# A convolution and attention hybrid: weighted sums two tiles behind, a norm in steps, leftovers at later pieces, a bias row on two row groups

## The chip, the core and the metric

The kernel runs on one core of a Trainium2 chip. A core has five engines with a queue each, which work at the same time and meet at semaphores: TensorE (PE in the profile, with its weight loads as PEld) multiplies matrices into PSUM, ScalarE (ACT) evaluates functions, VectorE (DVE) does elementwise work, reductions and 32x32 block transposes, GpSimd (POOL) does elementwise work and copies between partitions, SyncE (SP) issues most of the loads and stores. Each engine takes its instructions in order. SBUF has 128 partitions.

The metric is the device time of one execution in microseconds (us). A profile is one execution of its own; its times are read from the first instruction on.

## The reference

Input x is (4, 128, 64, 64): four images (N) of 128 channels and 4096 pixels, which later are tokens. Cut to what matters:

```python
# layer 0
g  = group_norm(x)                                   # 32 groups of 4 channels
e1 = prelu(w1 @ g + b1); e2 = prelu(w2 @ g + b2)     # 64 channels each
a  = prelu(wa @ g + ba)                              # 128 channels
x  = x + einsum('nij,ncj->nci', softmax(einsum('nci,ncj->nij', e1, e2), axis=2), a)
# layer 1, on tokens t: (4, 4096, 128)
u  = ln(t)
z  = cos(heads(u) + rx) and its running products     # 16 heads of 8
q  = ring(z)
ctx = softmax(q @ q.T / sqrt(8)) @ q                 # keys, queries and values are the same q
x1 = ln(u + ctx @ w_comb.T + b_comb)
f  = relu((cos(x1[..., :8]) * cos(ry)) @ f1.T + fb1) @ f2.T + fb2
t  = t + ln(x1 + f)
# layer 2: Wx = batch_norm(ln(t) @ W.T); y_k = sigmoid(Wx_k + y_(k-1) @ V.T); t = t + y
```

## The kernel before

**Stages.** The loop at the end of the kernel takes the images one after the other. For each, `first_stage` does layer 0 (`layer0`) and between its pieces the feed-forward of the image before; `second_stage` does the attention (`attention`). After the fourth image `third_stage` does the last feed-forward, and the recurrence over tokens follows. Inside the stages the order of the instructions on TensorE, ScalarE and VectorE is the order in which the code is written; in the attention that holds for GpSimd too. Where one stage follows another, a planner may mix the instructions of both ends.

**The convolutions.** `layer0` first normalises x (L327, eight parts), then makes e1 and e2 in eight pieces: two matmuls (L339) into a pair of PSUM banks, two activations on ScalarE (L291, L292), one operation on VectorE (L293). Then come four pieces of `asmT`: for each of two banks a bias matmul of one row (L347), then sixteen instructions of `wa` (L356) on top of it, then two operations on VectorE (L297, L298). After each of these twelve pieces, and after each score piece later, it calls `meanwhile`, which takes one leftover of the attention before, if there is any, a step of the image's own tokens, and a step of the feed-forward of the image before (`step_late`). A feed-forward is started on the first call and another every fifteen calls, at most two at a time. Its third step computes the statistics of `v`, with a power on GpSimd (r_v, in `rsqrt`, L225), and its fifth uses them on VectorE (L252).

**The attention.** Keys, queries and values are the same matrix, so the scores are symmetric, and the kernel computes each tile of 128 keys by 1024 queries only once where it can. For each of eight pairs of heads there are four blocks of 1024 queries. A block works through its own eight key tiles and through the tiles of the next one or two blocks: blocks 0 and 1 have 24 tiles (two foreign, one own, and so on), blocks 2 and 3 have 16 (one foreign, one own). Each tile is one turn of the loop (L823):

- scores: four matmuls on four row groups (L833) into two buffers of `ps_pair` (three in all);
- two exponentials on ScalarE (L842); for a foreign tile with a sum over the row (an accumulator read follows). The result goes into `exps` (six buffers) or into unused parts of `xs`, five turns deep;
- `run_pending`: mirror steps (L693), which use transposed foreign tiles as weights for the other block. Four foreign tiles make a group of sixteen steps; `credit` says how many are taken in a turn;
- `weigh` (L711): the weighted sum of the tile before, into the one accumulator of the block (`ps_acc`). After a block's last tile `finish` (L735) transposes the accumulator into `o` (L739), copies it on GpSimd into `own` (L747, sixteen copies) and puts two functions into `ends`: `mirrored` (`by_token` L732, `turned` L759 on VectorE, `other` L766 on GpSimd, sums into `own`) and `result` (reciprocal L773 and product L774 on VectorE);
- `run_flips`: transposes of foreign tiles on VectorE (L680), not on the last tile of a block.

At the end of an image the last two `result` functions are handed on as `left`. In the last block of an image three functions prepare the next one (`upcoming`): at the third tile the loads of x (`load_x`), at the fifteenth the eight `bn_stats` of `norm_stats` (L304) and their aggregate, and behind the last tile the two matmuls over groups (L309, L317) and the power r_g. `turned` has one buffer, `other` one of its own.

**Memory.** The stages' pools stand one behind another in SBUF from the left or the right. What a stage writes waits for the readers of what stood at the same place. In the attention, `queries`, `fixed` (q_aug and mirror), `keys` stand in this order; in an even image `flipped` stands at the right end.

Of the kernel before, what the change touches and what calls it, by code (L numbers as in the profile page):

```python
# [10 lines left out]
F32 = mybir.dt.float32  # L11
# [15 lines left out]
def kernel(  # L27
# [45 lines left out]
    TG = 4  # L73
# [84 lines left out]
    ba_row = load(ba, "ba_row")  # L158
# [141 lines left out]
    def norm_stats(n, xs):  # L300

        st = once.tile([P, NIC, 6], F32, tag="gst", name=f"gst{n}")
        for i in range(NIC):
            nc.vector.bn_stats(st[:, i, :], xs[:, ts(i, IC)])  # L304
        mv = once.tile([P, 2], F32, tag="gmv", name=f"gmv{n}")
        nc.vector.bn_aggr(mv, st)
        yield
# [7 lines left out]
        nc.vector.scalar_tensor_tensor(tv, dm, dm, mv[:, 1:2], ALU.mult, ALU.add)  # L315
        pv = get("ps_tok", f"pv{n}")
# [3 lines left out]
    def layer0(n, xs, xh, norm, shifted, begin, meanwhile):  # L320
# [23 lines left out]
        for i in range(NIC // 2):  # L344
            pc = pair_psum(f"pa{n}_{i}")
            for j in range(2):
                nc.tensor.matmul(  # L347
                    pc[:, j, :],
                    ones[0:1, :],
                    ba_row.unsqueeze(1).broadcast_to([1, TG, P]),  # L350
                    start=True,
                    stop=False,
                    skip_group_check=True,
                )
# [106 lines left out]
    def tokens(im, i, sums):  # L461
# [26 lines left out]
        by_token = small.tile([P, P], F32, tag="sums", name=f"sums{n}_{i}")  # L488
# [66 lines left out]
    def attention(n, q, xs, tail, upcoming):  # L555
# [152 lines left out]
        def weigh(it):  # L708
            for h in range(2):
                for x in range(2):  # L710
                    nc.tensor.matmul(  # L711
                        it["acc"][ts(2 * h + x, 32), :],
# [22 lines left out]
        def finish(pair, b, acc, later, denom):  # L735
# [3 lines left out]
            nc.vector.transpose(o, acc)  # L739
# [11 lines left out]
            def mirrored():  # L751
# [9 lines left out]
                other = once.tile([P, QT * 2 * D], F32, tag="other", name=f"other{n}_{pair}_{b}")  # L761
# [42 lines left out]
        before = None  # L804
# [8 lines left out]
        for pair in range(NPAIR):  # L813
            keys, queries, qa, later, denom = ready
            for b in range(NQB):
                acc = get("ps_acc", f"acc{n}_{pair}_{b}")
# [6 lines left out]
                for at, jt in enumerate(tiles):  # L823
# [30 lines left out]
                    if at == 1:  # L854
                        credit = max(credit, 3.0)
                    credit -= run_pending(turn, int(credit))
# [3 lines left out]
                    if before is not None:  # L860
                        weigh(before)
                        if before["last"]:
                            finish(*before["block"])
# [29 lines left out]
                    if jt != tiles[-1]:  # L893
                        run_flips(2)
# [3 lines left out]
                    if end_of_all and at in (2, QT + 6) and upcoming:  # L898
                        upcoming.pop(0)()
                    before = {  # L900
                        "acc": acc,
# [5 lines left out]
                        "block": (pair, b, acc, later, denom),  # L907
                    }
                assert not coming
# [3 lines left out]
        weigh(before)  # L913
        finish(*before["block"])
        while flips or pending:
            run_flips(TG)
            run_pending(turn + 2, 16)
        for f in upcoming:
            f()
# [217 lines left out]
    def first_stage(im, before):  # L1137
# [11 lines left out]
        with stage(f"conv{n}", **pools, **psum), tc.manual_schedule(engines=engines):  # L1149
            nc.vector.memset(get("gap", f"gap{n}")[:, 0:1], 0.0)  # L1150
            own = []
            step_late = in_steps(feed_forwards(before) if before else [], 15, 2)

            def meanwhile(steps=1):
                if before and before["left"]:
                    before["left"].pop(0)()
# [24 lines left out]
    def second_stage(im, tail, upcoming):  # L1181
# [3 lines left out]
            queries=((P, IC), 6),  # L1185
            fixed=((P,), 1),
            keys=((P, QB), 6),
# [4 lines left out]
            turned=((P, 2 * P), 1),  # L1192
# [6 lines left out]
        sides = {"flipped": "right"}  # L1199
        if im["side"] == "right":  # L1200
            sides = {}
# [48 lines left out]
    x_next = {"xs": load_x(0, ts(0, P))}  # L1250
    for n in range(N):
# [4 lines left out]
        upcoming = []  # L1256
        if n + 1 < N:
            upcoming = [
                lambda: x_next.update(xs=load_x(n + 1, ts(n + 1, P))),
                lambda: x_next.update(norm=norm_stats(n + 1, x_next["xs"])) or next(x_next["norm"]),  # L1260
                lambda: x_next.update(norm=next(x_next["norm"])),
            ]
# [112 lines left out]
    with tc.If(any_bad > 0):  # L1375
        with tc.For_i(0, N * P, P) as r0:
            image = open_image("r", ds(r0, P), "left", load_x("r", ds(r0, P)))
            second_stage(image, first_stage(image, None), [])
# [101 lines left out]
```

## Time and profile before

| | us |
|---|---|
| median of 3 runs (lowest, highest) | 7468.12 (7465.14, 7470.33) |
| the profiled execution's own time | 7473.21 |
| its span, first to last instruction | 7471.5 |
| mean granted clock of TensorE | 0.976 of full |

Among the costliest groups of instructions are:

| line, engine, what | count | busy us | mean ns |
|---|---|---|---|
| L842 ACT, exponentials into `exps` | 3144 | 3096.7 | 1036 |
| L842 ACT, exponentials into `xs` | 1976 | 1958.5 | 1036 |
| L680 DVE, transposes of foreign tiles | 3072 | 2221.8 + 1375.4 | 1216, 1214 |
| L693 PE, mirror steps | 49152 | 1867.8 | 279 |
| L711 PE, weighted sums | 20480 | 1683.9 + 1055.7 | 595, 594 |
| L833 PE, attention scores | 10240 | 1309.8 | 495 |
| L347 PE, bias of the value convolution | 64 | 42.9 | 802 |
| L304 DVE, statistics of x | 32 | 19.7 | 677 |

A line of a timeline gives the start and the length in us, the engine, the source line, the operation, the tile written and the tiles read, the shape, and how many instructions are merged; in brackets stands how long the engine was idle before and what ended that. Matmuls overlap, so for TensorE the distance from start to start says more than a length. A fp32 matmul counts as two instructions. A line of the waits gives the engine, what it was about to write, what it waited for, and the sum, the number and the longest of such waits. A window line gives the stretch, its length, the busy time of each engine with the instructions in it, the granted clock of TensorE (1.00 is full), the share of the DMA engines and GB/s.

### The profile page before, as it was taken

What the parts mean: (1) busy time and instruction counts of PE and PEld (TensorE: products, weight loads), DVE (VectorE), ACT (ScalarE), POOL (GpSimd) and SP (SyncE); (2) the same over time, 40 slices, a digit from 0 to 9 for tenths busy, and PEclk for the clock granted to TensorE, in tenths of its full rate; (3) what the DMA queues carried; (4) which work ended last, traced back from release to release, by engine and by line L of the source; (5) the groups of instructions that cost most, each with busy time, mean ns of one, the idle gap of its engine ahead of it and who ended that gap; (6) DMA issues with size and microseconds to landing.
All of it is one profiled execution on the core that took longest, in us unless ns stands there. A gap on an engine that the chain in (4) does not pass through costs nothing. (4 is left out here: it accounts for less than half of the span.)

```text
span 7471.5 us, 212466 instructions
## 1 busy us (share of the span) xinstructions
PE 7212.8 (97%) x88078; PEld 3317.1 (44%) x88078; DVE 5435.5 (73%) x7364; ACT 6104.6 (82%) x9557; POOL 2718.0 (36%) x9768
## 2 busy tenths in 40 slices
PE   8999999999999999999899999999999999999977
PEld 3434444444444444444444444444444444444446
DVE  4677777775777777777677777777667777777764
ACT  3479999995448999999344999999844599999975
POOL 1024443342224444343323433444322343444342
PEclk9999999999999999999899999999999999999978
DMA  0010000000111000000011100000001100000012
GB/s 26 26 43 22 23 25 21 19 9 22 36 45 37 26 19 21 23 23 17 15 36 46 36 21 19 23 24 18 18 20 40 43 30 21 23 23 26 11 58 102
DMA packets 81506, 211.99 MB, mean 28 GB/s; under 512 B 8769, under 2 KB 8801, under 8 KB 79761
## 3 DMA queue, kind: packets, MB, share of 16 engines
q1 hardware_dynamic: 77312, 186.68, 7.3%
q8 instruction: 693, 11.35, 0.6%
q10 hardware_dynamic: 2016, 10.49, 0.3%
q14 instruction: 285, 2.33, 0.1%
q0 software_dynamic: 1200, 1.14, 0.1%
HBM read 141.65 MB, written 56.62 MB: 27 GB/s over the span
## 5 line engine op out<-in xcount | busy, mean ns | idle before, releaser
L842 ACT ACTIVATE e<-s 128x1024 f32<-128x1024 f32 x3144 | 3096.7, 1036 | 25.3 <-PE s L833 15.2
L680 DVE STREAM_TRANSPOSE t<-e 128x1024 f32<-128x1024 f32 x1896 | 2221.8, 1216 | 496.0 <-ACT e L842 495.4
L842 ACT ACTIVATE xs<-s 128x1024 f32<-128x1024 f32 x1976 | 1958.5, 1036 | 17.5 <-PE s L833 5.5
L693 PE MATMUL misc<-t,mirror 128*32 128x128 f32 x49152 | 1867.8, 279 | 12.5 <-DVE later L704 11.4
L711 PE MATMUL acc<-e,q_aug 128*32 128x512 f32 x12576 | 1683.9, 595 | 0.0
L680 DVE STREAM_TRANSPOSE t<-xs 128x1024 f32<-128x1024 f32 x1176 | 1375.4, 1214 | 352.1 <-ACT xs L842 351.5
L693 PEld LDWEIGHTS misc<-t,mirror 128*32 128x32 f32 x49152 | 1200.2, 110 | 623.5 <-issue 598.8
L833 PEld LDWEIGHTS s<-queries,keys 32*128 32x128 f32 x10240 | 497.2, 182 | 2165.5 <-issue 1804.3
L747 POOL COPY own<-o 32x36 f32<-32x36 f32 x2048 | 428.3, 209 | 2622.3 <-DVE o L739 2542.3
L833 PE MATMUL s<-queries,keys 32*128 32x512 f32 x10240 | 1309.8, 495 | 17.2 <-ACT e L842 11.6
L711 PE MATMUL acc<-xs,q_aug 128*32 128x512 f32 x7904 | 1055.7, 594 | 0.0
L403 PE MATMUL acc<-p,asmT 128*128 128x512 f32 x2048 | 983.0, 612 | 0.0
L388 ACT ACTIVATE p<-s 128x1024 f32<-128x1024 f32 x512 | 497.1, 1022 | 569.3 <-PE s L380 562.3
L396 DVE TENSOR_TENSOR total<-total,p 128x1024 f32<-128x1024 f32 x448 | 575.7, 1285 | 296.8 <-ACT p L388 273.0
L650 POOL COPY mirror<-q 32x128 f32<-32x128 f32 x2048 | 604.8, 295 | 112.6 <-PE misc L693 22.9
L403 PEld LDWEIGHTS acc<-p,asmT 128*128 128x128 f32 x2048 | 360.9, 192 | 516.8 <-issue 514.5
L380 PE MATMUL s<-e,e 64*128 64x512 f32 x2048 | 524.2, 630 | 3.9 <-DVE asmT L298 3.7
L766 POOL COPY other<-turned 32x64 f32<-32x64 f32 x2048 | 470.7, 230 | 87.3
L711 PEld LDWEIGHTS acc<-e,q_aug 128*32 128x32 f32 x12576 | 396.1, 110 | 33.6 <-ACT e L842 18.9
L842 ACT ACTIVATION_READ_ACCUMULATOR e<-s 128x1 f32 x1896 | 406.5, 214 | 0.0
L380 PEld LDWEIGHTS s<-e,e 64*128 64x128 f32 x2048 | 180.8, 191 | 277.1 <-issue 262.3
L711 PEld LDWEIGHTS acc<-xs,q_aug 128*32 128x32 f32 x7904 | 249.3, 110 | 18.3 <-ACT xs L842 8.7
(243 smaller groups left out, 4742.9 us busy)
## 6 DMA issues: line engine op xcount, KB each, us to landing
keys<-parts_dram SPq DMA_DIRECT2D x256, 256.0 KB
queries<-parts_dram SPq DMA_DIRECT2D x1024, 32.0 KB
fx<-x_dram SPq DMA_DIRECT2D x64, 256.0 KB
x_dram<-x SPq DMA_DIRECT2D x56, 256.0 KB
xs<-in_x_dram SPq DMA_DIRECT2D x16, 512.0 KB
t_dram<-t2T SPq DMA_DIRECT2D x32, 256.0 KB
t2s<-t_dram SPq DMA_DIRECT2D x16, 512.0 KB
parts_dram<-high SPq DMA_DIRECT2D x28, 256.0 KB
```

Source lines behind the costliest of these rows:

```text
L380: nc.tensor.matmul(s[:, j, :], e2[rows, ts(2 * jp + j, P)], e1[rows, ts(ic, IC)], start=True, stop=True,)
L388: nc.scalar.activation(p, s, AF.Exp)
L396: nc.vector.tensor_tensor(state[ic], state[ic], p, ALU.add)
L403: nc.tensor.matmul(state["acc", ic], asmT[:, ts(2 * jp + j, P)], p[:, j, :], start=jp == 0 and j == 0, stop=jp == NP - 1 and j == 1,)
L650: nc.gpsimd.tensor_copy(wv[ts(a, 32), s, :, :, ts(a, D)], own[ts(s, 32)])
L680: nc.vector.transpose(group["e"][h][:, k, :], es[h])
L693: nc.tensor.matmul(state["acc"][ts(2 * h + x, 32), :], state["w"][:, QT * (s // 4) + TG * x + s % 4, h, :], state["e"][h][:, :, ds(IC * x ...
L711: nc.tensor.matmul(it["acc"][ts(2 * h + x, 32), :], it["qa"][:, ds((2 * it["jt"] + h) * V, 32)], it["e"][h][:, ts(x, IC)], start=it["first ...
L747: nc.gpsimd.tensor_copy(own[ts(s, 32), ts(x, 4), h, :], ov[ts(2 * h + x, 32), s, :, 0:V])
L766: nc.gpsimd.tensor_copy(to[ts(k, 32), h], tv[ts(2 * h + x, 32), k])
L833: nc.tensor.matmul(ss[h][:, x, :], keys[jt // QT].bitcast(F32R)[r, cols], queries[b].bitcast(F32R)[r, :], start=True, stop=True,)
L842: nc.scalar.activation(es[h], ss[h].rearrange("p x c -> p (x c)"), AF.Exp, scale=1.0 / math.sqrt(D), accum_out=denom[:, slot, jt, h : h + ...
```

## The change

1. The bias row is loaded at partitions 0 and 32, and the two bias matmuls of a piece use one each, so that they lie on two row groups.
2. `norm_stats` yields after each `bn_stats` and once between its two group matmuls. `upcoming` becomes a generator: the loads of x at the third tile of the last block, a step at the ninth tile and every one after it, one per round of the loop that empties what is pending behind the last tile, and the rest.
3. Tiles go into a list `waiting`; a tile is weighed two turns after its exponentials, ahead of the turn's mirror steps. The accumulator is taken at the block's first weighted sum, and `finish` gets the block instead of the accumulator.
4. `run_flips` is left out on the first tile of a block, not on the last.
5. The leftovers are taken at the tenth and the eleventh call of `meanwhile` instead of the first and the second.
6. `turned` has two buffers, and `other` is one of them; `by_token` of `tokens` has one buffer instead of two. `keys` stands before `fixed`; in an even image `keys` stands at the right end, and `flipped` doesn't.

```diff
-    ba_row = load(ba, "ba_row")
+    ba_row = const.tile([33, P], F32, tag="ba_row", name="ba_row")
+    for i in range(2):
+        nc.gpsimd.dma_start(out=ba_row[ds(32 * i, 1), :], in_=ba)
...
             nc.vector.bn_stats(st[:, i, :], xs[:, ts(i, IC)])
+            yield
         mv = once.tile([P, 2], F32, tag="gmv", name=f"gmv{n}")
         nc.vector.bn_aggr(mv, st)
-        yield
...
         nc.vector.scalar_tensor_tensor(tv, dm, dm, mv[:, 1:2], ALU.mult, ALU.add)
+        yield
...
-                    ones[0:1, :],
-                    ba_row.unsqueeze(1).broadcast_to([1, TG, P]),
+                    ones[ds(32 * j, 1), :],
+                    ba_row[ds(32 * j, 1), :].unsqueeze(1).broadcast_to([1, TG, P]),
...
-        by_token = small.tile([P, P], F32, tag="sums", name=f"sums{n}_{i}")
+        by_token = once.tile([P, P], F32, tag="sums", name=f"sums{n}_{i}")
...
         def weigh(it):
+            if it["first"]:
+                it["in"]["acc"] = get("ps_acc", "acc{}_{}_{}".format(n, *it["block"]))
...
-                other = once.tile([P, QT * 2 * D], F32, tag="other", name=f"other{n}_{pair}_{b}")
+                other = get("turned", f"other{n}_{pair}_{b}")[:, 0 : QT * 2 * D]
...
                         credit = max(credit, 3.0)
+
+                    if len(waiting) == 2:
+                        it = waiting.pop(0)
+                        weigh(it)
+                        if it["last"]:
+                            finish(*it["block"])
                     credit -= run_pending(turn, int(credit))
                     turn += 1
                     while ends and ends[0][0] < turn:
                         ends.pop(0)[1]()
-                    if before is not None:
-                        weigh(before)
-                        if before["last"]:
-                            finish(*before["block"])
...
-                    if jt != tiles[-1]:
+                    if at:
                         run_flips(2)
...
-                    if end_of_all and at in (2, QT + 6) and upcoming:
-                        upcoming.pop(0)()
+                    if end_of_all and (at == 2 or at >= QT):
+                        next(upcoming, None)
...
-        weigh(before)
-        finish(*before["block"])
+        for it in waiting:
+            weigh(it)
+        finish(*it["block"])
         while flips or pending:
+            next(upcoming, None)
             run_flips(TG)
             run_pending(turn + 2, 16)
-        for f in upcoming:
-            f()
+        for _ in upcoming:
+            pass
...
-                if before and before["left"]:
+                calls[0] += 1
+                if before and calls[0] in (10, 11):
                     before["left"].pop(0)()
...
             queries=((P, IC), 6),
+            keys=((P, QB), 6),
             fixed=((P,), 1),
-            keys=((P, QB), 6),
...
-            turned=((P, 2 * P), 1),
+            turned=((P, 2 * P), 2),
...
-        sides = {"flipped": "right"}
-        if im["side"] == "right":
-            sides = {}
+        sides = {"keys": "right"} if im["side"] == "left" else {}
...
+    def prepare_image(n):
+        x_next.update(xs=load_x(n, ts(n, P)))
+        yield
+        for step in norm_stats(n, x_next["xs"]):
+            x_next["norm"] = step
+            yield
```

## The prediction

> **What bounds the kernel.** I read the busy totals first, then the timeline inside the attention, the timeline where one image ends and the next begins, the waits, and last the windows with the granted clock. The totals name no single engine:
>
> ```profile
> PE 7212.8 (97%) x88078; PEld 3317.1 (44%) x88078; DVE 5435.5 (73%) x7364; ACT 6104.6 (82%) x9557; POOL 2718.0 (36%) x9768
> ```
>
> The run has four equal images. By the first and last exponential (L842) of each, the four attention stages last 1277.5, 1275.1, 1275.3 and 1274.2 us, 5102 us of the 7471.5. The stretches before them are 447 us for image 0 and 546.5, 554.5 and 550.3 us for the others, which carry the previous image's feed-forward as well. About 270 us follow the last attention.
>
> Inside the attention, TensorE's timeline reads (start, length, instructions merged):
>
> ```profile
> 1011.14 0.50 PE L833 MATMUL s<-queries,keys 32*128 32x512 f32 x4
> 1011.57 0.86 PE L693 MATMUL misc<-t,mirror 128*32 128x128 f32 x24
> 1012.25 1.04 PE L711 MATMUL acc<-xs,q_aug 128*32 128x512 f32 x8
> 1013.22 0.50 PE L833 MATMUL s<-queries,keys 32*128 32x512 f32 x4
> 1013.65 0.86 PE L693 MATMUL misc<-t,mirror 128*32 128x128 f32 x24
> 1014.34 1.04 PE L711 MATMUL acc<-xs,q_aug 128*32 128x512 f32 x8
> 1015.30 0.51 PE L833 MATMUL s<-queries,keys 32*128 32x512 f32 x4
> ```
>
> Start to start: scores 0.43 us, mirror steps (8 instructions each) 0.22 us a step, weighted sum 0.97 us. No row waits. A turn with three steps takes 2.09 us, one with two 1.87. In the same stretch ScalarE starts its two exponentials 0.995 us apart where an accumulator read follows and 0.903 apart where none does: 1.99 us a turn for a foreign tile, 1.81 for an own one. Blocks 0 and 1 of a pair repeat "foreign, foreign, own" with eight steps in three turns: TensorE needs 3 x 1.42 + 8 x 0.22 = 6.0 us, ScalarE 5.8, and the rows repeat every 6.04. They are TensorE's. Blocks 2 and 3 alternate foreign and own: ScalarE needs 8 x (1.99 + 1.81) = 30.4 us a block, TensorE with about 33 steps 30.0, and they last 30.8 and 31.0. They are ScalarE's. The two engines are almost in balance, so the attention has little to give.
>
> Where image 0 ends (its last exponential ends at 1724.81):
>
> ```profile
> 1724.31 4.80 DVE L304 BATCH_NORM_STATS2 gst<-xs 128x6 f32<-128x512 f32 x8
> ...
> 1729.71 5.37 PE L693 MATMUL misc<-t,mirror 128*32 128x128 f32 x128 [3.80 <-DVE later L704]
> ...
> 1736.90 0.56 POOL L225 TENSOR_TENSOR r_g<-v_g,minus_half 128x1 f32<-128x1 f32 x1 [2.53 <-DVE v_g L223]
> ...
> 1738.09 3.78 PE L339 MATMUL pca<-q,w_sb 128*128 128x512 f32 x4 [1.54 <-DVE q L327]
> ...
> 1746.79 0.45 DVE L759 STREAM_TRANSPOSE turned<-later 128x256 f32<-128x256 f32 x1 [7.39 <-POOL other L766]
> ...
> 1758.60 0.25 DVE L773 RECIPROCAL inv<-own 128x16 f32<-128x16 f32 x1 [8.30 <-POOL own L769]
> ```
>
> Eight statistics hold VectorE, so TensorE waits to finish the mirror sums; the next image's first convolution starts 13.3 us after the last exponential; then VectorE stands 7.39 us for the second turned tile and 8.30 us for the leftover result, the convolutions' activations queued behind both. The value convolutions (L347) begin at 1769.3, 44.5 us after the last exponential; for the other two images the distance is 48.2 and 45.2 us. In the waits:
>
> ```profile
> DVE inv L773 <- POOL own L769: 56.7, 66, 13.1
> DVE turned L759 <- POOL other L766: 37.3, 4, 15.1
> ```
>
> Last, the value convolutions themselves, by windows (first line: all engines, from PE busy on, then the clock; second line: image 0, the bias matmuls L347 alone):
>
> ```profile
> 54.60:70.70 16.10, 16.10 (x48) 10.34 (x47) 5.02 (x4) 0.00 (x0) 0.00 (x0) 0.50 0.01 1
> ```
> ```profile
> 45.90:70.70 24.80, 11.52 (x16) 3.64 (x16) 0.61 0.00 1
> ```
>
> TensorE has no gap there and yet half its clock. The stage lasts 24.8, 22.2, 24.1 and 22.2 us in the four images, and the one-row bias matmuls hold 11.52, 9.77, 11.77 and 9.83 us of it, 42.9 together.
>
> **Bias on two row groups.** Each of 16 pieces (4 per image) has two bias matmuls, one after the other: 1.98 us at full clock, 3.78 at half. The nearest row for two row groups at once is the convolution scores L380 (64 rows each): eight instructions start in 1.99 us, where eight full-height ones of L403 take 3.70. So half the 42.9 us goes: -21.4. From both sides: nothing if the pair still runs in turn; if the clock stays full as well, a piece takes 0.95 (half its bias) + 2.05 (L356 at full clock) = 3.0 us, four of them with VectorE's 2.5 us on the last some 14.3, and four images 57 instead of 93.3: -36. I take -25, close to the halving, because how much of the clock comes back no row shows. The second copy of the bias row is one more load on GpSimd's queue, which is what the first group matrix waits behind (loads 0.53 us apart up to 22.7): +0.5.
>
> The Trainium skill (TensorE: Matmul & The Clock Gate, section "Why this matters for your kernels") holds that TensorE stays at full clock as long as there are no idle gaps over about 3 us. By it this stage would be at full clock already and the halving worth 16 x 0.95 = 15 us. The window above (busy 16.10 of 16.10, clock 0.50) contradicts it, so I keep the measured 42.9.
>
> **The norm in steps.** Eight `bn_stats` (0.6 us apart) move into the last eight turns. In those turns VectorE sits idle 1.45 to 1.5 us before each pair of transposes, one pair per two turns, and two statistics take 1.2: hidden, three images. Uncovered they would cost what they cost now, 4.8. x's four loads start at 1698.05 as before, perhaps one turn later because weighted sums read the old contents one turn longer; the busy DMA share ends at about 1709, and the first statistics fall at 1694 + 8 x 1.93 = 1709.5: nothing, at worst some 2 us an image. After the last exponential the chain is then: weighted sum 1.0, `o` transpose 0.7, aggregate 0.4, the group matmul at +2.3, a second at +3.3; GpSimd's 16 copies (4.0) end at +5.9, its power at +6.5; 16 last mirror steps (3.5 us at full clock) end near +8, the accumulated copy precedes the normalisation on VectorE, and the first convolution starts at about +9 instead of +13.3: 4.3 us, and what is late next is the GpSimd chain.
>
> **Leftovers at calls 10 and 11.** GpSimd's chain after the last exponential is 4.0 (own) + 0.6 + 4.5 (by token) + 5.3 (other) + 5.5 + 5.3 = 25, ending at +28 where it now ends at +34. The reciprocals (two of 0.25, two products of 0.29) then run at about +40: no wait. But the wait does not vanish. `turned` still waits for the earlier one's readers (two buffers, but `other` takes every second), at about +15.6 instead of +22. And the feed-forward's first power r_v (2 us) queues on GpSimd behind the chain, until +29.5; its reader L252 is the fifth call's, in VectorE's order ahead of pieces 6 to 8. So: pieces at ScalarE's 2.2 us from +18, held from +26 to +30.7, end at +34.5: 10 us earlier than +44.5. Three images: -30, of which the norm has 13. Bounds: 4.3 x 3 = 13 if the queue takes all back; 60 if r_v does not hold VectorE and the eight pieces follow at 2.2 us from +9 (18 us, +27, 17.5 us each, with some clock).
>
> **Weighted sums two tiles late.** Every turn issues the same 4 + 8 + steps instructions, now scores, weighted sum, steps. In blocks 0 and 1 TensorE never waits, so nothing comes back. In blocks 2 and 3 what lies above ScalarE's own time is 0.4 + 0.6 = 1.0 us a pair; 32 pairs make 32 us at best. I take half, 0.5 x 32 = -16, since the stall at a block's start (`o` before the one accumulator is reused) stays. A loss: the switch from weighted sum to scores costs 0.11 us, into the steps 0.02, and each is still made once a turn, so nothing by that; a misjudged 0.01 us a turn over 2560 turns would be 26 either way.
>
> The rule that speaks against it, from the skill (TensorEngine Tiling, "Key Properties"), is that a change of tiling mode drains TensorE; a third change per turn would have cost 2560 x 0.11 = 280 us by the measured drain. Weighted sum and steps share 128x32, so there are two as before.
>
> `finish` comes one turn later, between the last weighted sum and the first of the next block stand three steps and the scores (1.2 us) as before. Skipping transposes on the first tile rather than the last keeps VectorE free for `o`. Keys in another place free the first image's loads: TensorE waited once 3.1 us for keys; -2.
>
> **Sum.** -25 + 0.5 - 30 - 16 - 2 = -72.5. The profiled execution's own time is 7473.2 (span 7471.5); less 72.5 is 7400.7. It lies 5.1 above the median of the runs, so **7395 us** is predicted.
>
> **Rivals.** (1) GpSimd's queue gives the transition back: only 13 there, 21 for the bias, nothing for the lag: 7468 - 34 = 7434. For it: every wait of the transition ends at POOL. Against: r_v is one wait in place of two. Chance 0.25. (2) The clock recovers: 36 + 60 + 32 = 128 less, about 7340; the 0.50 window speaks for it, the 31 us of thin TensorE work before it against. 0.13. (3) The bias pair runs in turn and the queue gives the rest back: 7455 to 7483, no difference. 0.07. (4) Slower: the one accumulator. `o` now starts in turn 1; if one transpose (1.2 us) stands ahead of it on VectorE, TensorE stalls at each of 128 block starts. VectorE now idles at least 0.57 us before `o`, and 0.2 us more are left before the next sum; from 0.6 us of stall a start (72/128) the gain is gone, at 1.2 it is 128 x 1.2 = 154 against 72, about 7550. 0.10. My forecast, 7375 to 7415, has 0.45.
>
> A measurement of this kernel tells some 0.2% (15 us) from no change. Faster: 0.45 + 0.25 + 0.13, rounded down to 0.81; within 0.08; slower 0.11. The range 7340 to 7462 leaves out rival 4 and the ends of 2 and 3.
>
> **What would show it.** L347 near 21 us with starts in pairs, value stage near 17 us an image; first convolution 9 us after the last exponential; L773 no longer waiting, a wait of L252 for r_v in its place; pairs still 157 us apart. A pair over 158 us, or TensorE waiting for `o`, would prove it wrong.

## The result, and the profile after

| | before | after |
|---|---|---|
| median of the runs (lowest, highest) | 7469.23 (7465.14, 7478.52), 4 runs | 7413.44 (7410.7, 7416.25), 4 runs |
| the profiled execution, its span | 7473.21, 7471.5 | 7414.47, 7412.7 |
| mean granted clock | 0.976 | 0.984 |

The ratio is 0.9924, 95% interval 0.9906 to 0.9941: 56 us less. The forecast was 7395 in a range of 7340 to 7462. After the change most line numbers are 3 to 6 higher (the exponentials are L848, the bias L351, `turned` L765, the reciprocal L779).

The next table cuts both profiled executions at the same events: the last exponential of an image, the first convolution matmul after it, the first bias matmul, the first score of the convolutions' attention. It is worked out from the start times in the two traces, for images 0, 1, 2, 3, in us:

| stretch | before | after | difference |
|---|---|---|---|
| last exponential to first bias matmul (images 1 to 3: the seam) | 44.5, 48.2, 45.3 | 33.7, 33.8, 33.7 | -36.8 |
| of that, to the first convolution | 13.3, 14.2, 14.1 | 8.1, 8.1, 8.1 | -17.3 |
| value stage, first bias matmul to first score | 24.8, 22.2, 24.1, 22.2 | 12.2, 19.7, 18.7, 22.8 | -19.9 |
| attention, first to last exponential | 1277.5, 1275.1, 1275.3, 1274.2 | 1274.5, 1274.1, 1275.4, 1275.6 | -2.5 |
| all else (start, scores to attention, tail) | | | +0.4 |

The sum, -58.8, is the difference of the spans. The attention is 68% of the run and gave nothing that stands out.

The busy totals after are:

```profile
PE 7153.2 (96%) x88078; PEld 3385.8 (46%) x88078; DVE 5395.9 (73%) x7364; ACT 6107.7 (82%) x9557; POOL 2730.3 (37%) x9769
```

TensorE lost 60 us of busy time with exactly as many instructions. 21.8 of them are the bias matmuls (42.9 us busy before, 21.1 after); the rest was not taken apart. The timeline at the end of image 0 (start, length, engine, line; the last exponential ends at 1710.10, so that 1718.20 is +8.1):

```profile
1706.43 1.24 DVE L307 BATCH_NORM_STATS2 gst<-xs 128x6 f32<-128x512 f32 x2
...
1712.37 0.35 PE L312 MATMUL pg<-gmv,grp 128*128 128x1 f32 x2 [1.16 <-DVE gmv L310]
...
1712.65 3.70 PE L697 MATMUL misc<-t,mirror 128*32 128x128 f32 x128
...
1717.01 0.56 POOL L228 TENSOR_TENSOR r_g<-v_g,minus_half 128x1 f32<-128x1 f32 x1 [0.93 <-DVE gap L1161]
...
1718.20 1.98 PE L343 MATMUL pca<-q,w_sb 128*128 128x512 f32 x4 [1.54 <-DVE q L331]
...
1726.90 0.45 DVE L765 STREAM_TRANSPOSE turned<-later 128x256 f32<-128x256 f32 x1 [7.39 <-POOL other L772]
...
1741.33 1.28 DVE L296 SCALAR_TENSOR_TENSOR e<-zb,a_sb,yb 128x1024 f32<-128x1024 f32 x1 [3.05 <-POOL own L774]
...
1743.52 1.11 DVE L255 TENSOR_SCALAR v<-v,mv_v,r_v 128x128 f32<-128x128 f32 x4 [0.91 <-POOL r_v L228]
...
1743.82 1.13 PE L351 MATMUL pa<-ba_row,ones 1*128 1x512 f32 x4 [1.41 <-ACT zb L295]
...
1754.35 2.08 PE L351 MATMUL pa<-ba_row,ones 1*128 1x512 f32 x4 [4.21 <-DVE asmT L301]
...
1756.57 0.24 DVE L779 RECIPROCAL inv<-own 128x16 f32<-128x16 f32 x1
```

The statistics now lie between transposes, and the reciprocal no longer waits here. VectorE's longest wait in this stretch, 7.39 us, still ends at GpSimd (POOL), and so do those of 3.05 and 0.91 us just ahead of the value stage; one of 3.05 us for the last mirror sums, not shown, ends at TensorE. Two of those on GpSimd were foreseen (`turned`, r_v); the one of `e` for `own` was not. In piece 3 of the value stage TensorE then waits 4.21 us for VectorE; that the late `e` is the reason is argued from the order on VectorE. The waits of the whole run (engine, what it was about to write, what it waited for, sum, number, longest):

```profile
DVE o L745 <- PE acc L717: 200.2, 125, 2.9
...
DVE inv L779 <- POOL own L775: 153.3, 93, 13.1
...
DVE turned L765 <- POOL other L772: 37.3, 4, 15.1
...
DVE e L296 <- POOL own L774: 9.5, 3, 3.4
...
DVE v L255 <- POOL r_v L228: 2.7, 3, 0.9
```

The reciprocal's wait for `own` has grown over the whole run, from 56.7 to 153.3 us. All but one of these waits (13.1 us behind the last attention, as before) lie inside the attention and are at most 1.8 us long, and the attention is no longer for it.

In image 0 nothing of an attention stands before the value stage, and there the change shows undisturbed (a window: the stretch, its length, busy time of PE, PEld, DVE, ACT, POOL with their instructions, then the clock):

```profile
46.10:59.20 13.10, 13.07 (x84) 8.87 (x84) 10.12 (x9) 4.07 (x4) 0.00 (x0) 1.00 0.00 1
```

The clock is 1.00 where it was 0.50, and the stage lasts 12.2 us instead of 24.8.

### The profile page after: what moved, and what is told of

Same layout as the page of the kernel before. It is cut to its first block, busy times and chain, and to the rows that moved or that the text cites. A ratio compares the mean times of both kernels' runs of the same rounds, so it can differ in the third digit from the quotient of the medians.

```text
span 7412.7 us, 212494 instructions
## 1 busy us (share of the span) xinstructions
PE 7153.2 (96%) x88078; PEld 3385.8 (46%) x88078; DVE 5395.9 (73%) x7364; ACT 6107.7 (82%) x9557; POOL 2730.3 (37%) x9769
## 5 line engine op out<-in xcount | busy, mean ns | idle before, releaser
L848 ACT ACTIVATE e<-s 128x1024 f32<-128x1024 f32 x3144 | 3102.2, 1042 | 24.2 <-PE s L839 12.5
L697 PEld LDWEIGHTS misc<-t,mirror 128*32 128x32 f32 x49152 | 1449.2, 110 | 1482.2 <-issue 1453.2
L848 ACT ACTIVATE xs<-s 128x1024 f32<-128x1024 f32 x1976 | 1960.5, 1040 | 13.3 <-PE s L839 2.3
L697 PE MATMUL misc<-t,mirror 128*32 128x128 f32 x49152 | 1801.0, 273 | 0.0
L839 PE MATMUL s<-queries,keys 32*128 32x512 f32 x10240 | 1372.8, 495 | 16.9 <-ACT e L848 15.5
L839 PEld LDWEIGHTS s<-queries,keys 32*128 32x128 f32 x10240 | 535.4, 181 | 607.9 <-issue 279.5
L654 POOL COPY mirror<-q 32x128 f32<-32x128 f32 x2048 | 604.2, 295 | 107.4 <-PE misc L697 19.7
L717 PEld LDWEIGHTS acc<-e,q_aug 128*32 128x32 f32 x12576 | 250.2, 108 | 387.5 <-issue 379.0
L848 ACT ACTIVATION_READ_ACCUMULATOR e<-s 128x1 f32 x1896 | 418.7, 221 | 0.0
L717 PEld LDWEIGHTS acc<-xs,q_aug 128*32 128x32 f32 x7904 | 156.3, 108 | 242.0 <-issue 226.3
```

Source lines behind the costliest of these rows:

```text
L654: nc.gpsimd.tensor_copy(wv[ts(a, 32), s, :, :, ts(a, D)], own[ts(s, 32)])
L697: nc.tensor.matmul(state["acc"][ts(2 * h + x, 32), :], state["w"][:, QT * (s // 4) + TG * x + s % 4, h, :], state["e"][h][:, :, ds(IC * x ...
L717: nc.tensor.matmul(it["in"]["acc"][ts(2 * h + x, 32), :], it["qa"][:, ds((2 * it["jt"] + h) * V, 32)], it["e"][h][:, ts(x, IC)], start=it[ ...
L839: nc.tensor.matmul(ss[h][:, x, :], keys[jt // QT].bitcast(F32R)[r, cols], queries[b].bitcast(F32R)[r, :], start=True, stop=True,)
L848: nc.scalar.activation(es[h], ss[h].rearrange("p x c -> p (x c)"), AF.Exp, scale=1.0 / math.sqrt(D), accum_out=denom[:, slot, jt, h : h + ...
```

## The experiments

Theory: the bias pair and the clock that it frees, the norm in steps and the later leftovers make the gain; the lag of the weighted sums makes little or none, because where it acts no engine was waiting for it. Rivals: the lag brings what the prediction gave it (16 us); or the gain in the seams is one thing alone, so that the parts don't add. "Before" beside each median is the kernel before on the same chip.

**1. The bias alone** (kernel before, with item 1 of the change).

```diff
-                    ones[0:1, :],
-                    ba_row.unsqueeze(1).broadcast_to([1, TG, P]),
+                    ones[ds(32 * j, 1), :],
+                    ba_row[ds(32 * j, 1), :].unsqueeze(1).broadcast_to([1, TG, P]),
```

> The kernel before with the bias on two row groups alone. If the bias explains the value convolutions by itself, the stage from the first bias matmul to the first score takes about 12 us in image 0 (24.8 before, 12.2 with the whole change), L347 starts in pairs and holds about half of its 42.9 us, and the clock in image 0's stage is full; the four images together give 20 to 40 us, so 7430 to 7450. If the full clock of image 0 came from another part of the change, its stage stays above 18 us and the gain is under 15 us.

7443.41 us (7438.41 to 7444.14) against 7469.42; ratio 0.9962 [0.9948, 0.9977]. The value stages are 12.2, 16.4, 16.4 and 16.3 us, the bias matmuls busy for 4.5 to 4.8 each, the seams are those of before (45.4, 47.0, 44.8). So the bias alone is worth 26 us. In the whole change the same stages of images 1 to 3 are 19 to 23 us: TensorE waits there for VectorE, up to 4.21 us at once, and part of each stage runs at half the clock (mean granted clock 0.83, 0.82 and 0.73).

**2. The lag alone** (kernel before, with items 3 and 4).

```diff
+                    if len(waiting) == 2:
+                        it = waiting.pop(0)
+                        weigh(it)
...
-                    if before is not None:
-                        weigh(before)
...
-                    if jt != tiles[-1]:
+                    if at:
```

> The kernel before with the lag of two tiles alone (and the transposes left out on the first tile instead of the last). If the two engines of the attention are balanced turn by turn through the number of mirror steps, the four attention stages stay at 1274 to 1278 us, blocks 0 and 1 at 48.3 and 2 and 3 at 30.6 to 31.0, and the time is within 5 us of before. If the lag is worth what was predicted, each stage is 4 us shorter and the time 16 us less; if it works at the seam between images, the stretch after the last exponential is shorter there.

7466.06 us (7461.7 to 7476.99) against 7469.42; ratio 0.9994 [0.9985, 1.0004]. The attention stages are 1278.7, 1276.0, 1276.7 and 1276.3 us, where they were 1277.5, 1275.1, 1275.3 and 1274.2. No gain is to be seen.

**3. The bias at full height** (kernel before). The row divided by 128 stands on all 128 partitions and is multiplied by ones: the same sum, as many matmuls as before, one after the other, each using 128 rows instead of one.

```diff
-    ba_row = load(ba, "ba_row")
+    ba_row = load_row(ba, "ba_row")
+    nc.vector.tensor_scalar(ba_row, ba_row, 1.0 / P, None, ALU.mult)
...
-                    ones[0:1, :],
-                    ba_row.unsqueeze(1).broadcast_to([1, TG, P]),
+                    ones,
+                    ba_row.unsqueeze(1).broadcast_to([P, TG, P]),
```

> The kernel before with the bias matmul at full height: the row divided by 128 stands in all 128 partitions and is summed by a matrix of ones. The number and the width of the matmuls stay, only the rows in use differ (128 for 1). If one-row matmuls are what lets the granted clock fall, image 0's stage runs at the full clock and takes about 4 x 4.0 = 16 to 17 us instead of 24.8, and the four images together some 20 to 30 us less. If the clock falls for another reason, such as waits, the stage stays at 22 to 25 us and the time at that of before.

7442.74 us (7438.07 to 7444.26) against 7469.42; ratio 0.9962 [0.9948, 0.9976]: as much as the two row groups give. Its timeline in image 0:

```profile
50.06 1.88 PE L348 MATMUL pa<-ba_row,ones 128*128 128x512 f32 x4
51.78 1.95 PE L357 MATMUL pa<-wa_sb,q 128*128 128x128 f32 x16
53.57 1.88 PE L348 MATMUL pa<-ba_row,ones 128*128 128x512 f32 x4
```

The bias matmuls still run in turn, 1.72 us from start to start of the next group instead of 1.06 with two row groups, but in image 0 nothing falls to half rate (granted clock 1.00 over the stage): value stages of 14.2, 15.2, 16.0 and 15.2 us instead of 24.8, 22.2, 24.1 and 22.2. Of the 12.6 us that image 0 won with two row groups, 10.6 come without any pair. Most of that is the clock: four pieces of one-row matmuls in turn at full rate would take 4 x (1.92 + 1.98) = 15.6 us, an estimate from the full-rate rows of before, so some 9 us are the clock and some 3.5 the pair.

**4. The norm in one go** (kernel after, without item 2's steps).

```diff
             nc.vector.bn_stats(st[:, i, :], xs[:, ts(i, IC)])
-            yield
...
-                    if end_of_all and (at == 2 or at >= QT):
+                    if end_of_all and at in (2, QT + 6):
```

> The changed kernel with the norm of the next x as before: all eight statistics at the fifteenth tile, the rest behind the last. If the norm in steps is worth what was worked out, the first convolution starts about 12 to 13 us after the last exponential again instead of 8.1, three times, and the time is 10 to 16 us above the changed kernel (7423 to 7430). If GpSimd's chain sets the end of the seam all the same, the value convolutions start no later than 34 us after the last exponential and the time is that of the changed kernel.

7429.82 us (7427.88 to 7431.16) against 7469.42; ratio 0.9945 [0.9929, 0.9962], 16.4 us above the changed kernel's 7413.44. The first convolution is back at +13.3, +11.6 and +13.3 us; the seams are 38.9, 37.2 and 38.9, 13.8 more in sum. The value stages of images 1 to 3 are 22.8 us each, 7 more in sum.

**5. The leftovers early** (kernel after).

```diff
-                if before and calls[0] in (10, 11):
+                if before and calls[0] in (1, 2):
```

> The changed kernel with the leftovers taken at the first and second call again. If GpSimd's chain sets the seam and the later call only swaps one wait of VectorE for another (the reciprocal's for that of r_v), the value convolutions start 1 to 4 us later than 33.7 us after the last exponential, three times, and the time is 3 to 12 us above the changed kernel. If the later call is the main gain of the seam, they start 8 us later or more and the time is 25 us above it.

7420.55 us (7415.19 to 7421.26) against 7469.08; ratio 0.993 [0.9914, 0.9947], 7 us above 7413.44. The seams are 39.7, 40.4 and 39.6 us, 18.5 more in sum and 6 us each, between the two cases of the expectation; but the value stages are 18.5, 14.0 and 18.7, 10 less. Moving the leftovers wins 18 us ahead of the value stages, and 10 are given back in them.

**6. The lag of one inside the whole change** (kernel after).

```diff
-                    if len(waiting) == 2:
-                        it = waiting.pop(0)
-                        weigh(it)
...
                     while ends and ends[0][0] < turn:
                         ends.pop(0)[1]()
+                    if waiting:
+                        it = waiting.pop(0)
+                        weigh(it)
```

> The changed kernel with the weighted sums one tile behind again, after the mirror steps, and the transposes left out on a block's last tile. From the lag alone, which moved nothing, the same is expected here: attention stages of 1274 to 1278 us and a time within 5 us of the changed kernel. If the lag helps only together with the norm in steps (the last tiles' sums and the statistics at the seam), the first convolution starts later than 8.1 us after the last exponential and the time is 5 to 15 us above it.

7411.44 us (7407.72 to 7415.28) against 7469.08; ratio 0.9919 [0.9902, 0.9935]. The attention stages are 1271.5, 1274.2, 1273.5 and 1275.7, 4.7 us less in sum than after. The second tile of lag is worth nothing either way.

**7. Fewer mirror steps early, more later** (kernel after). Blocks 0 and 1 are TensorE's, so steps were put off from them into blocks 2 and 3.

```diff
-                    rates = (2.9, 2.2) if len(behind[b]) == 2 else (2.2, 1.9)
+                    rates = (2.75, 2.0) if len(behind[b]) == 2 else (2.5, 2.1)
```

> The changed kernel with other rates for the mirror steps: 2.75 and 2.0 a turn instead of 2.9 and 2.2 in blocks 0 and 1, 2.5 and 2.1 instead of 2.2 and 1.9 in blocks 2 and 3, so that some four steps a block move from where TensorE sets the time to where ScalarE does. If the balance of steps is what is left in the attention, blocks 0 and 1 take 47.4 to 47.8 us instead of 48.4, blocks 2 and 3 at most 0.5 us more each, a pair is 0.5 to 1.5 us shorter and the time 15 to 45 us less than the changed kernel's. If some other wait holds the attention, pairs stay at 158 us.

7448.62 us (7443.77 to 7450.79) against 7469.08; ratio 0.9973 [0.9962, 0.9984]: 35 us slower than the changed kernel, a miss. By median starts, blocks 0 and 1 last 47.54 and 47.53 us instead of 48.45 and 48.35, as hoped; block 2 lasts 33.23 instead of 30.58, and block 3 31.21 instead of 30.96. Its timeline in the third turn of block 2, and its waits:

```profile
1015.85 4.58 DVE L684 STREAM_TRANSPOSE t<-e 128x1024 f32<-128x1024 f32 x4
...
1020.36 0.68 DVE L745 STREAM_TRANSPOSE o<-acc 128x512 f32<-128x512 f32 x1
...
1021.09 1.06 PE L717 MATMUL acc<-xs,q_aug 128*32 128x512 f32 x8 [1.43 <-DVE o L745]
...
1023.06 2.96 ACT L848 ACTIVATE e<-s 128x1024 f32<-128x1024 f32 x3 [1.23 <-PE s L839]
```
```profile
PE acc L717 <- DVE o L745: 40.1, 28, 1.4
```

Four transposes without a gap stand ahead of `o` on VectorE; the weighted sum that opens the next block waits 1.43 us for the one accumulator, the scores behind it come late, and ScalarE waits for them. That happens 28 times, 40 us in sum, about half of what block 2 loses (2.65 us in each of 32 pairs); the other half was not traced. It is the mechanism of the fourth rival, and in the changed kernel TensorE never waits in this way: there it is only the weight load that waits for `o`, 0.2 us at the longest.

**8. A second buffer for `turned`, and the feed-forward paused in calls 3 to 7** (kernel after).

```diff
-                other = get("turned", f"other{n}_{pair}_{b}")[:, 0 : QT * 2 * D]
+                other = once.tile([P, P], F32, tag="sums", name=f"other{n}_{pair}_{b}")
...
-                step_late()
+                if not 2 < calls[0] < 8:
+                    step_late()
```

> The changed kernel with two things at the seam: other has a place of its own again (that of the sums), so that the two turned tiles use two buffers, and the feed-forward takes no step at calls 3 to 7, so that its power r_v comes when GpSimd's chain has ended. If these two waits on GpSimd are what is left of the seam, VectorE no longer waits 7.4 us for turned nor for r_v, the eight pieces take 18 to 20 us instead of 25.6, and the time is 10 to 25 us below the changed kernel. If the delay comes back at the end of the convolutions, because the feed-forward ends five calls later, the time is that of the changed kernel.

7495.35 us (7490.49 to 7496.93) against 7469.08; ratio 1.0034 [1.0022, 1.0047]: 82 us slower than after. The seams are 33.6 us, as in the changed kernel: the eight pieces did not get shorter, VectorE now waits 7.37 us for `by_key` and 6.51 for `other`. The value stages are indeed 14.1, 15.5 and 14.1; but from the scores to the attention it takes 512.6, 511.2 and 512.9 us, where it took 482.6, 482.6 and 480.7. Five calls without a feed-forward step cost 30 us an image at the other end; by the code, what is left of the feed-forwards is run to its end there, ahead of the attention. The 17.5 us won in the value stages cost five times as much there.

**9. The second buffer alone** (kernel after).

```diff
-                other = get("turned", f"other{n}_{pair}_{b}")[:, 0 : QT * 2 * D]
+                other = once.tile([P, P], F32, tag="sums", name=f"other{n}_{pair}_{b}")
```

> The changed kernel, with `other` moved out of the pair of `turned` buffers into the single buffer of `sums`, so that the second transposed tile `turned` need not wait until GpSimd has read out the one before it. Nothing else differs. If that wait (7.39 us of VectorE in each of three seams, the rows `turned <- other`) holds the activations behind it, the value stages begin up to 7 us earlier (26 to 30 us after the last exponential, where it was 33.7) and the run is 10 to 20 us faster than the changed kernel's 7413. If the wait is only passed on, because the sums' result then waits for GpSimd's copies and the feed-forward's power instead, the wait of 7.39 us is gone from the profile, another row of VectorE waiting for GpSimd grows by about as much, and the time stays within 5 us of 7413.

7416.01 us (7413.64 to 7420.8) against 7467.94; ratio 0.9931 [0.9918, 0.9945]: no change. The timeline says where the wait went:

```profile
1716.67 0.40 DVE L765 STREAM_TRANSPOSE turned<-later 128x256 f32<-128x256 f32 x1
1717.13 3.74 DVE L331 TENSOR_SCALAR q<-xs,gm,r_g 128x512 f32<-128x512 f32 x8
1728.23 2.48 DVE L296 SCALAR_TENSOR_TENSOR e<-za,a_sb,ya 128x1024 f32<-128x1024 f32 x2 [7.37 <-POOL by_key L731]
...
1740.45 1.56 DVE L296 SCALAR_TENSOR_TENSOR e<-zb,a_sb,yb 128x1024 f32<-128x1024 f32 x1 [4.95 <-POOL other L772]
```

`turned` no longer waits and the normalisation runs through; now `e` waits, 7.37 us where `turned` waited 7.39, for the next step on GpSimd. By the profile it is a read of `denom`, the attention's buffer; that `e` lies where the attention's buffers stood, and so waits for their last readers, fits it but is inferred. Whatever VectorE comes to first stands until GpSimd has gone through its chain.

**10. The same with a lag of one** (kernel after, with the diffs of runs 6 and 9 together).

> As the run before it, and with the weighted sums one tile late as they were before the change. The lag moved nothing in two runs: expected within 4 us of the run beside it, attention stages of 1271 to 1276 us. If the lag is worth what the prediction gave it, it is 16 us slower.

7414.38 us (7413.63 to 7419.66) against 7467.94; ratio 0.9929 [0.9915, 0.9942]; attention stages of 1273.6 to 1275.7. A third time the lag makes no difference.

**11. GpSimd's chain shortened** (kernel after). At the end of an image alone, the 2 x 16 small copies of `by_token` go to ScalarE and the addition ahead of them to VectorE.

```diff
-                nc.gpsimd.tensor_tensor(by_key, total, denom[:, slot, ts(b, QT), :], ALU.add)
+                eng = nc.vector if over else nc.gpsimd
+                eng.tensor_tensor(by_key, total, denom[:, slot, ts(b, QT), :], ALU.add)
...
-                    nc.gpsimd.tensor_copy(dst[ts(s, 32), a], src[ts(a, 32), s])
+                    copy = nc.scalar.copy if over else nc.gpsimd.tensor_copy
+                    copy(dst[ts(s, 32), a], src[ts(a, 32), s])
...
+        over.append(1)
         first[0]()
```

> The changed kernel, with one thing moved at the three seams alone: the 2 x 16 small copies that turn the sums by key into sums by token leave GpSimd for ScalarE, and the one addition ahead of them goes to VectorE. In the changed kernel they hold GpSimd for 4.5 + 6.1 us between the last exponential and the fifth convolution piece, while ScalarE stands idle for 10.1 us. Theory: what sets the seam and the start of the value stage is GpSimd's chain of leftovers (own 4.0, power 0.6, by token 4.5, other 4.7, by token 6.1, other 6.7, power 2.0; its last product ends 31 us after the last exponential). Then VectorE's wait for `other` (7.4) falls to about 3, the later ones for `own` and r_v go, the value convolutions begin 26 to 30 us after the last exponential (33.7 now), their stage falls from 19-23 to 14-17 us, and the run is 25 to 40 us faster than the changed kernel: 7375 to 7390. Rival: the seam is set by something else (ScalarE's two halves of each piece, TensorE's clock), or what is won is given back later as in the run with the paused feed-forward: 7405 to 7420. A loss is possible where a ScalarE copy takes more than some 0.3 us: 32 of them would then end after +10 and hold the first convolution's activations.

7385.05 us (7381.95 to 7389.02) against 7468.62; ratio 0.9889 [0.9873, 0.9906]: 28 us below the changed kernel by the medians, and the fastest of all. Its timeline at the end of image 0 (last exponential at +0 = 1708.8):

```profile
1708.63 3.28 ACT L740 COPY by_token<-denom 32x4 f32<-32x4 f32 x16
...
1716.10 3.25 ACT L740 COPY by_token<-by_key 32x4 f32<-32x4 f32 x16 [4.20 <-DVE by_key L732]
...
1716.25 2.72 POOL L774 COPY other<-turned 32x64 f32<-32x64 f32 x8
...
1719.38 1.11 ACT L294 ACTIVATE ya<-pca,b_sb 128x1024 f32<-128x1024 f32 x1
...
1731.60 0.23 POOL L777 TENSOR_TENSOR own<-own,by_token 128x16 f32<-128x16 f32 x1
1731.82 1.98 POOL L228 TENSOR_TENSOR r_v<-v_v,minus_half 128x4 f32<-128x4 f32 x1
```

ScalarE takes its copies ahead of the first activation, in time that it had idle but for 0.4 us, and GpSimd is through with r_v at +25.0 instead of +33.4. The seams are 28.3 us each (-16.3 in sum), the value stages of images 1 to 3 are 14.3, 19.2 and 16.0 (-11.7), and the stretch behind the last attention, where the same leftovers stand, 262.2 instead of 269.2. So GpSimd's chain set the seam: shown, by shortening it. The value stages are less sure: the same code takes 14.3 to 19.2 us in the three images, by the clock (last section).

**12. The same with the second buffer for `turned`** (kernel after, with the diffs of runs 9 and 11 together).

> As the run beside it, and with `other` in a buffer of its own, which moved nothing while GpSimd's chain was long (7416), because the wait only passed on to the next step of that chain. With the chain 10 us shorter the wait left over (about 3 us in each seam) may count by itself: 0 to 9 us faster than the run beside it. If the wait passes on again, the same time.

7386.97 us (7382.99 to 7391.42) against 7468.62; ratio 0.9891 [0.9875, 0.9908]. The seams lose another 1.6 us each (26.7), the value stages of images 1 to 3 (22.0, 17.9 and 18.8) take 9 us more: no difference in the time.

## Why the prediction was right, and where it was off

The likeliest case came: faster, 7413 where 7395 was forecast, at the edge of that case's own range (7375 to 7415). By spans -72.5 was forecast and -58.8 measured. The 13.7 us between them are 15.5 too much for the attention (-18 for lag and keys against -2.5), 5.1 too much for the value stages (-25 against -19.9) and 6.8 too little for the seams (-30 against -36.8).

**Bias: the size right, in part by luck.** -25 was forecast; alone the part gives 26.0. L351 is busy for 4.5, 5.5, 4.7 and 6.4 us, 21.1 in sum, as written ("near 21"), and its four instructions take 1.13 us at full clock. But the sum got its -25 from the pair, half of 42.9, with a little clock on top, and the pair was the smaller cause: run 3 has no pair and wins 26.7 us. The part was chosen between a halving (-21.4) and a halving with a full clock (-36), "because how much of the clock comes back no row shows": all of it came back in image 0, where the stage went from 24.8 to 12.2, below the 14.3 worked out for that end. In the whole change images 1 to 3 take 18.7 to 22.8, with TensorE waiting for VectorE. Why VectorE is behind there was not shown. The shorter seam by itself is not the reason: in run 4, with seams of 37 to 39 us, all three stages take 22.8, and in run 8, with 33.6, they take 14.1 to 15.5.

**Seam: the place right, the count wrong, the end partly luck.** First convolution at +9, measured +8.1; value stage at +34.5, measured +33.7 to +33.8; `turned` still waiting, measured 7.39 us; no wait for the reciprocal any more; L255 waiting for r_v, measured but small (0.9 three times), because the wait for `own` just ahead of it takes 3.05 of the 4.7 us foreseen. GpSimd was slower than forecast: its chain was done at +31.4 (forecast +28) and r_v at +33.4 (+29.5), the second `by_token` taking 6.11 us where the first took 4.49. The value stage still began near the forecast +34.5, because by its row it hung on `zb`, which waited for the `e` of +31.2 and not for r_v. Too small was "10 us earlier than +44.5. Three images: -30": the text itself gives 48.2 and 45.2 for the other two seams, and 34.5 taken from these would have given -34.4. The parts, each undone by itself: norm 16 us (13 forecast), 13.8 of them within the seams; leftovers 18 us within the seams (17 forecast), of which 10 are lost in the value stage. The first rival had said that GpSimd's queue gives the transition back; it came true for those 10 of 36.8 us at most, in another stage.

**Lag: a term that was not there.** "I take half, 0.5 x 32 = -16" is the step that failed. The lag moves nothing: 7466 against 7469 alone, 7411 against 7413 inside the change, 7414 against 7416 beside the second buffer; pairs last 158.3 us before and after (the median distance of their first scores); the prediction's "pairs still 157 us apart" was too low, and its sign of being wrong, "a pair over 158 us", held before the change already and says nothing. The 1.0 us a pair that lies above ScalarE's own time in blocks 2 and 3 is real, but it isn't the wait that a lag removes: counted per turn, the mirror steps are the same before and after, and the longer turns (1.95 to 2.10 us instead of 1.81) are the own tiles on which `credit` lets three or four steps through. The accounting said that TensorE and ScalarE are nearly in balance, and the forecast still charged the remainder to a wait that no row showed. The other term of the attention, -2 for the keys, fits: the 3.1 us that TensorE waited for the first image's keys are gone, and that image's attention is 3.0 us shorter.

**The slower rival** did not come, and its mechanism is real: in run 7 a redistribution of steps is enough for VectorE to stand four transposes ahead of `o`, and TensorE loses 40 us in 28 stalls. The chance given to it rested on a margin of 0.57 us; that margin held in the changed kernel and not in its neighbour.

**The clock rival** (7340) asked for a full clock everywhere. It came in image 0, not behind the attentions: there TensorE waits up to 4.21 us within the value stage, and the piece that follows the wait shown runs at half rate (L351 2.08 us instead of 1.13).

**Open.** The parts measured alone or undone are 26 (bias), 16 (norm), 7 (leftovers) and 0 (lag), 49 of 56. The keys' place, `turned` with two buffers and `by_token` with one were not undone alone. The lengths of stages come from one profile of each kernel, and those of the value stages move by some us with the clock.

## What to carry to other kernels

When an engine's wait ends at another engine, ask what that engine's whole queue holds from the last event on: freeing one buffer (run 9) only passed the same 7.4 us to the next instruction, while taking 10 us of small copies out of the queue (run 11) brought 28. A remainder of busy time over span is worth a forecast only if a row shows an engine waiting for what the change moves. And a seam's saving is to be counted from each seam's own row, with the stage behind it asked whether it can begin earlier.

## What the runs showed of the hardware

**Matmuls of one row let the clock fall though TensorE has no gap.** Before, it was granted 0.50 in a stretch of 16.1 us that it was busy throughout. With the same matmuls at 128 rows (run 3) image 0's stage keeps full rate (clock 1.00; 1.88 and 1.95 us in the rows shown). With two one-row matmuls side by side, 35% of the piece's time instead of half of it (1.06 of 3.04 us; in turn, at full rate, 1.92 of 3.9), the clock was 1.00 as well.

**After a real gap the clock was down too, and a short one may do.** In the timeline after, TensorE's 4.21 us of idle time are followed by one bias group of 2.08 us. The Trainium skill (TensorE: Matmul & The Clock Gate, section "Why this matters for your kernels") advises to leave no idle gaps above some 3 us between bursts. This row agrees with it; the window of before shows a second cause that this advice does not name. And in run 11 TensorE's longest gap within the value stage is 1.67 or 1.68 us in images 1 to 3, and yet the clock (the number behind POOL's) was full in one and not in the others:

```profile
1737.10:1751.40 14.30, 12.62 (x84) 9.06 (x84) 13.89 (x21) 3.57 (x4) 2.57 (x2) 1.00 0.00 0
3538.40:3557.50 19.10, 17.42 (x84) 12.72 (x84) 13.98 (x21) 3.57 (x4) 2.57 (x2) 0.73 0.00 1
5343.60:5359.50 15.90, 14.22 (x84) 10.59 (x84) 13.86 (x21) 3.54 (x4) 2.55 (x2) 0.89 0.00 1
```

The work is the same, 84 matmul instructions each. What decides between them no run shows.

**A GpSimd copy that starts during a VectorE instruction with two inputs in SBUF lasts until that instruction ends.** In the profile of run 11:

```profile
1724.41 1.27 DVE L296 SCALAR_TENSOR_TENSOR e<-za,a_sb,ya 128x1024 f32<-128x1024 f32 x1
...
1724.62 1.16 POOL L774 COPY other<-turned 32x64 f32<-32x64 f32 x1
...
1725.81 0.23 POOL L774 COPY other<-turned 32x64 f32<-32x64 f32 x1
1726.03 1.29 DVE L296 SCALAR_TENSOR_TENSOR e<-za,a_sb,ya 128x1024 f32<-128x1024 f32 x1 [0.36 <-ACT za L295]
...
1726.09 1.33 POOL L774 COPY other<-turned 32x64 f32<-32x64 f32 x1
```

The copy between the two takes 0.23 us, the two that fall into L296 take 1.16 and 1.33. In this trace all nine such copies that start during L296 take 1.16 to 1.33 us and end 0.1 us after it; beside a block transpose they take 0.23. So VectorE's work in the seam lengthens the chain that it waits for. The Trainium skill (GPSIMD Engine Reference, section "1. Specifications") says that GpSimd shares its SBUF interfaces with VectorE, with contention where VectorE reads two SBUF inputs; these rows agree.

**A small copy costs as much on ScalarE.** The 32x4 copies of `by_token` have a median of 192 ns on ScalarE (run 11) and of 182 on GpSimd (after); at the end of image 0 sixteen of them in a row take 3.28 and 3.25 us on ScalarE and 4.5 and 6.1 on GpSimd.
